# Fixed PSUM pairs with a planned slot per product, and score blocks in two clusters of four, in a two-layer graph attention kernel

## The chip, the cores and the metric

The kernel runs on one core of a Trainium2 chip (trn2). The metric is the device time of one execution in microseconds. The kernel before took 2311.61 us, the median of three runs (2310.8 to 2316.13).

## What is computed

64 graphs of 256 nodes with 512 features go through two layers, all in fp32. Cut to what matters, for one graph:

```
# layer 0
p = x @ fc_w.T + fc_b
l = (p @ q_w + q_b)[:, None] + (p @ k_w + k_b)[None, :]
l = leaky_relu(l + (1 - adj) * -1e9, 0.01)
x = softmax(l) @ p + x
# layer 1, 8 heads of 64, the layer's "adjacency" is the same adj
Q, K, V = x @ W_q + b_q, x @ W_k + b_k, x @ W_v + b_v
s = Q K^T / 8 + (x @ w_g[:D])[:, None] + (x @ w_g[D:])[None, :] + b_g + log(adj + 1e-9)
out = softmax(s) V + x
```

## The kernel before

**Groups and steps.** Two graphs make a group (512 tokens, four tiles of 128), so there are 32 groups and 32 steps. The function `step` (its pieces are strings such as `"pq.p7 pq.p2"`) works on four groups at once: `f` is the group whose layer 0 ends and whose projections to Q, K and V are made; `a` is the group before it, in its attention; `d` is the one before `a`, whose second graph is finished; `n` is the next one, which is loaded and whose layer-0 weights are made. The order of the pieces in these strings is the order in which each engine gets its instructions: a manual schedule keeps it, and every engine runs its queue in order. So the strings in `attention_and_layer_0` and `step` are what decides which instruction stands behind which.

**Products.** Each 512 x 512 x 512 product (`pq`, `pk`, `pv` for the projections, `pf` for layer 0) is made of seven products of blocks, `p1` to `p7` (class `Product`, `add` at L412). One block product is four matmuls of 128x256 with a contraction of 128; the profile shows two records for each fp32 matmul, so 8 records. `p1`, `p2` and `p7` start a new PSUM bank (`fresh`); `p6`, `p5` and `p3` add to `p1`'s bank, and `p4` adds to `p7`'s. Between them the bank is read: `keep_1`, and the `keep` inside `p6` and `p5`, copy it on ScalarE (L429, or L432 as two halves with a bias; for `pf` L494 as two halves with a factor, followed by an addition on GpSimd, L495). `p3`'s result is read by ScalarE (for `pf` by VectorE). `sum_00`, `sum_11` and `sum_10` read a bank on VectorE (L443; for `pf` L501).

**Layer 0.** `mix:0` to `mix:3` make `y` (L689), four products of 8 records, each copied to SBUF by ScalarE (L695). `recip` makes row sums on TensorE (L637). `residual` (L830) is four ScalarE instructions that prepare x plus the bias for the output; `turn_residual` turns it on VectorE.

**Attention.** `scores:u` for u = 0 to 3 (one graph and four of its heads each) makes two score blocks, jc = 0 and 1, one for each 128 of the graph's nodes. A block is four matmuls (L859) with a contraction of 64, two at a time on the two halves of the array's rows; it fills two banks, and one exp on ScalarE (L873) reads both. `factor:u:jc` multiplies the exp by the adjacency on VectorE (L879), `both:u` adds the two blocks (L886). `attend:gr` makes V times weights for one graph (L899): two halves of 8 matmuls with 64 output columns, two at a time on halves of the array's columns; each half fills one bank, which ScalarE copies (L906). `totals_0` is a small matmul for the sums (L927).

**PSUM before.** There are eight banks. Four of them turn in a pool of single banks (`ps`, 4 buffers), which every block product, `y` and `attend` takes from in order of need; the other four are a pool of two pairs (`psc`), which the score blocks and `pq.p7` take in turn:

```
def bank(name):
    return ps.tile([P, 512], F32, tag="bank", name=name)

def pair(name):
    return psc.tile([P, 2, 512], F32, tag="pair", name=name)
```

The framework sets the waits between engines from what each instruction reads and writes, tile by tile.

**Order before, around the attention.** On TensorE: `pv.p5`, `scores:0`, `attend:1` (of `d`), `scores:1`, `pv.p3`, `pv.p4`, `mix:0`, `mix:1`, `recip`, `mix:2`, `mix:3`, `pf.p1`, `p2`, `p6`, `p7`, `p5`, `p3`, `scores:2`, `attend:0`, `totals_0`, `scores:3`, `pf.p4`, then `pq.p1`, `pk.p1`, `pv.p1`, `pq.p6`, `p7`, `p2`, `p5`, `pk.p6`, `pq.p3`, `p4`, `pk.p7`, `p5`, `p2`, `p3`, `p4`, `pv.p2`, `p6`, `p7`, `p5`.

Of the kernel before, what the change touches and what calls it, by code (L numbers as in the profile page):

```python
# [17 lines left out]
P = 128  # L18
# [7 lines left out]
def kernel(  # L26
# [119 lines left out]
    def transposed_weights(w, pool, psum, copy):  # L146

        t = pool.tile([P, NC, D], F32, tag="fcT", name="fcT")
        for hc in range(NC):
            pt = psum.tile([P, 512], F32, tag="bank", name=f"pfc_{hc}")  # L150
            for oc in range(NC):
                nc.tensor.transpose(pt[:, ts(oc, P)], w[:, oc, ts(hc, P)], ident)
            copy(t[:, hc, :], pt)
        return t
# [9 lines left out]
    def fast():  # L164
        main = ExitStack()
        with main:
# [6 lines left out]
                tc.tile_pool(name="ps", bufs=4, space=bass.MemoryType.PSUM)  # L173
            )
            psc = main.enter_context(
                tc.tile_pool(name="psc", bufs=2, space=bass.MemoryType.PSUM)
            )

            def bank(name):
                return ps.tile([P, 512], F32, tag="bank", name=name)  # L180

            def pair(name):
                return psc.tile([P, 2, 512], F32, tag="pair", name=name)
# [61 lines left out]
            def columns(rows, cols, name):  # L245

                n = rows.shape[0]
                pt = bank(name)
                nc.tensor.transpose(pt[:, 0:n], rows, ident[0:n, 0:n])
                nc.vector.tensor_copy(cols, pt[:, 0:n])  # L250
# [6 lines left out]
            def rows_of_x():  # L257

                pr = bank("rows_qk")[0:2, :]
                for oc in range(NC):  # L260
                    nc.tensor.matmul(
                        pr, lhsT=cols_0[:, oc : oc + NC + 1 : NC], rhs=fc_nat[:, oc, :],
                        start=(oc == 0), stop=(oc == NC - 1),
                    )
                rows = one.tile([2, D], F32, tag="junk", name="rows_qk_sb")
                nc.scalar.copy(rows, pr)
                return rows

            def spread_rows(rows):

                for n, dst in enumerate((wq_row, wk_row)):
                    pt = bank(f"row_{n}")
                    nc.tensor.matmul(
                        pt, lhsT=ident[0:2, n : n + 1].to_broadcast([2, P]), rhs=rows,
                        start=True, stop=True,
                    )
                    nc.scalar.copy(dst, pt)

            def constant():

                both = two.tile([P, NC], F32, tag="c", name="qk_col")
                part = two.tile([P, 2, T], F32, tag="kq", name="qk_fcb")
                nc.vector.tensor_tensor(both, qw_col, kw_col, ALU.add)
                nc.vector.tensor_tensor(both, both, fcb_col, ALU.mult)
                nc.vector.tensor_reduce(part[:, 0, 0:1], both, AX.X, ALU.add)
                pk = bank("pk")
                nc.tensor.matmul(
                    pk[:, 0:1], lhsT=part[:, 0, 0:1].to_broadcast([P, P]), rhs=ones[:, 0, 0:1],
                    start=True, stop=True,
                )  # L290
                return lambda: nc.vector.scalar_tensor_tensor(
                    kqc, pk[:, 0:1], qb, kb, ALU.add, ALU.add
                )

            def constants_of_projections():


                pc = bank("pc")[:, 0:HALF]
# [11 lines left out]
                def add():  # L310
                    pt = bank("pct")
# [77 lines left out]
            class Product:  # L389
# [5 lines left out]
                scores = False  # L395

                def __init__(self, name, a, b, out, rows, bias=None):
                    self.name, self.a, self.b, self.out = name, a, b, out
                    self.rows, self.bias = rows, bias
# [18 lines left out]
                def fresh(self, n, scores=False):  # L418
                    name = f"{self.name}_{n}"
                    dst = (pair(name)[:, 0] if scores else bank(name)).rearrange(  # L420
                        "p (m k) -> p m k", m=2
                    )
                    self.add(n, dst, True)
                    return dst
# [36 lines left out]
                def p7(self):  # L461
                    self.r2 = self.fresh(7, self.scores)
# [66 lines left out]
            class Group:  # L529


                older = None

# [43 lines left out]
                def queries(self):  # L577

                    pt = bank(f"qrow_{self.g}")
# [52 lines left out]
                def recip(self):  # L632
# [3 lines left out]
                    all_sums = bank(f"rc_{self.g}")[:, 0:ALL]  # L636
# [15 lines left out]
                def sums(self):  # L652

                    sm = bank(f"sm0_{self.g}")[:, 0:P]
# [10 lines left out]
                def recip_of_sums(self):  # L665
                    pt = bank(f"rc_{self.g}")[:, 0:P]
                    nc.tensor.transpose(pt, self.sms, ident)
                    nc.vector.reciprocal(
                        recip0[:, self.g, :], pt.rearrange("p (t r) -> p t r", t=T)[:, :, 0]
                    )  # L670

                def mix(self, c):
# [13 lines left out]
                    y = bank(f"y_{g}_{c}")  # L686
# [10 lines left out]
                def features_first(self):  # L697
# [4 lines left out]
                    for t in range(T):  # L702
                        pt = bank(f"xTp_{g}_{t}")
# [7 lines left out]
                    fcT = transposed_weights(fc_nat, wts, ps, nc.scalar.copy)  # L711
# [3 lines left out]
                    def product(t):  # L715
                        pp = bank(f"fp_{g}_{t}")
# [29 lines left out]
                    for t in range(T):  # L746
                        gr, ic = divmod(t, TPG)
                        po = bank(f"x1p_{g}_{t}")
# [16 lines left out]
                def begin(self):  # L765
# [19 lines left out]
                    self.pq.scores = True  # L785
# [21 lines left out]
                def x1t(self, t):  # L807

                    pt = bank(f"x1Tp_{self.g}_{t}")
# [37 lines left out]
                def scores(self, u):  # L847
# [5 lines left out]
                    for jc in range(TPG):  # L853
                        t = gr * TPG + jc
                        sc = pair(f"sc_{g}_{u}_{jc}").rearrange("p a (b i) -> p a b i", b=2)
# [32 lines left out]
                def attend(self, gr):  # L888
# [3 lines left out]
                    for hg in range(2):  # L892
                        po = bank(f"oT_{g}_{gr}_{hg}")
# [40 lines left out]
                def totals_1(self):  # L934
                    self.totals(1, bank(f"tot_{self.g}_1")[:, 0 : NC * N // B])

                def totals_0(self):
                    self.totals(0, bank(f"tot_{self.g}_0")[:, 0 : NC * N // B])
# [16 lines left out]
                def sums_1(self, gr):  # L955
# [3 lines left out]
                    sm = bank(f"sm_{g}_{gr}")[:, 0:N]  # L959
# [11 lines left out]
                def sums_of_e(self, gr):  # L971

                    g = self.g
                    sm = bank(f"sm_{g}_{gr}")[:, 0:N]
# [93 lines left out]
            def attention_and_layer_0(D, A, F, X):  # L1068

                A("scores:0")  # L1070
                D("attend:1")
                F("add_tiles")
                A("scores:1 factor:0:0 factor:0:1 pv.sum_11 pv.p3 pv.p4")
                D("turn:1")
                F("parts_0")
                A("factor:1:0 factor:1:1 pv.sum_10 both:0 both:1")
# [8 lines left out]
                A("scores:2 attend:0 totals_0")  # L1085
                F("pf.sum_01 send:0:1 fetch:1:1 fetch:0:1")
                F("copy:0")
                A("factor:2:0 factor:2:1 scores:3 turn:0 ratios:0 both:2")
                F("pf.p4 pf.sum_10 send:1:0 fetch:1:0")
                F("pq.p1 pq.keep_1 pk.p1 pk.keep_1 pv.p1 pv.keep_1")  # L1090

            def check_ranges():

                in_range(NG - NR // 2, NG, "last")
                pk = bank("pok")
# [11 lines left out]
            def step(d, a, f, n, check):  # L1107
# [24 lines left out]
                A("factor:3:0 factor:3:1 both:3")  # L1132
# [18 lines left out]
                if n is None:  # L1151
                    A("attend:1 totals_1 ratios:1 turn:1 divide:1 complete:1 store:1")
# [17 lines left out]
            with tc.manual_schedule(engines=ENGINES):  # L1170
# [3 lines left out]
                warm = bank("warm")  # L1174
# [17 lines left out]
    def general(pool):  # L1192
# [12 lines left out]
        with tc.tile_pool(name="gwps", bufs=2, space=bass.MemoryType.PSUM) as wps:  # L1205
            fcT = transposed_weights(fc_nat, pool, wps, nc.vector.tensor_copy)
# [199 lines left out]
```

## Time and profile before

| what | value |
|---|---|
| time, median of 3 runs (range) | 2311.61 us (2310.8 to 2316.13) |
| span of the profiled execution | 2308.8 us |
| TensorE busy, matmul records | 2294.2 us (99%), 12618 records |
| VectorE busy | 2124.2 us (92%) |
| ScalarE busy | 1071.8 us (46%) |
| GpSimd busy | 121.9 us (5%) |
| mean granted TensorE clock | 0.997 |
| HBM read and written over the span | 70 GB/s |

The span runs from the first to the last instruction of one execution; the times of the runs have what is outside the span as well, some 2.8 us. Busy time is the union of an engine's records. PE is TensorE's matmuls, PEld its weight loads, DVE VectorE, ACT ScalarE, POOL GpSimd, SP the engine that issues most DMAs. In a line of the timeline the columns are: start, length (both us), engine, line of the kernel, operation, what is written <- what is read, shapes, number of instructions merged, and in square brackets the idle time of that engine before it and what ended it. Ends of matmuls are modelled and reach over the start of the next one, so the distance of two starts, not the length, is a matmul's price.

### The profile page before, as it was taken

How to read it: one execution, taken by the hardware profiler on the slowest of the kernel's cores; microseconds unless marked ns; L12 is line 12 of the kernel's file. 1: busy time of each engine (PE TensorE's matmuls, PEld its weight loads, DVE VectorE, ACT ScalarE, POOL GpSimd, SP SyncE). 2: the span in 40 equal slices, each digit the busy share in tenths (PEclk: the TensorE clock that was granted, in tenths of full speed). 3: DMA queues.
4: the chain of work that ended last, by engine and by line, in shares of the span. 5: the costliest groups of instructions: out<-in, count | busy, mean ns of one | idle time of the engine just before them, and what ended most of it. 6: DMA issues, size and time to landing. Idle time of an engine off the chain costs nothing.

```text
span 2308.8 us, 33613 instructions
## 1 busy us (share of the span) xinstructions
PE 2294.2 (99%) x12618; PEld 1905.2 (83%) x12618; DVE 2124.2 (92%) x3180; ACT 1071.8 (46%) x1865; POOL 121.9 (5%) x120
## 2 busy tenths in 40 slices
PE   9999999999999999999999999999999999999997
PEld 6888888888888888888888888888888888888885
DVE  6899999999999999999999999999999999999997
ACT  3544444454445444454444454444544445444443
POOL 0000000000000000000000000000000000000000
PEclk9999999999999999999999999999999999999999
DMA  4122332223322233232233232332222323223312
GB/s 133 46 61 73 78 76 66 70 61 85 79 73 61 61 78 78 74 68 61 69 78 83 60 75 63 79 78 74 64 60 74 78 73 70 65 64 81 84 46 38
DMA packets 517264, 163.84 MB, mean 71 GB/s; under 512 B 415188, under 2 KB 478696, under 8 KB 517096
## 3 DMA queue, kind: packets, MB, share of 16 engines
q1 hardware_dynamic: 514440, 160.32, 28.8%
q8 instruction: 102, 1.67, 0.3%
q10 hardware_dynamic: 2656, 1.31, 0.2%
q14 instruction: 66, 0.54, 0.1%
HBM read 95.43 MB, written 66.12 MB: 70 GB/s over the span
## 4 chain that ended last, share of the span: by engine, by line
PE 98%; DVE 1%; DMA 0%; ACT 0%; issue 0%; ACTq 0%; DVEq 0%
PE pv L412 17%; PE pq L412 17%; PE pf L412 16%; PE pk L412 16%; PE sc L859 11%; PE oT L899 10%; PE y L689 9%; PE fp L718 1%; DMA fc_nat<-in_L_gnn_fc_w_dram 0%; PE rc L637 0%; DVE osb L1034 0%; PE tot L927 0%; DVE osb L1040 0%; PE xTp L705 0%; DVE osb L1033 0%; DVE x L756 0%
## 5 line engine op out<-in xcount | busy, mean ns | idle before, releaser
L873 ACT ACTIVATE e<-sc,c 128x1024 f32<-128x1024 f32 x254 | 269.0, 1110 | 79.2 <-PE sc L859 77.6
L879 DVE TENSOR_TENSOR e<-e,am 128x1024 f32<-128x1024 f32 x254 | 297.7, 1213 | 0.4 <-ACT e L873 0.4
L859 PE MATMUL sc<-qT,kT 64*128 64x256 f32 x2048 | 255.8, 390 | 0.3 <-ACT e L873 0.3
L899 PE MATMUL oT<-e,v 128*64 128x256 f32 x2032 | 233.4, 382 | 0.0
L859 PEld LDWEIGHTS sc<-qT,kT 64*128 64x128 f32 x2048 | 187.3, 187 | 52.6 <-issue 32.7
L495 POOL TENSOR_TENSOR pf_s<-pf_s,x 128x512 f32<-128x512 f32 x93 | 118.4, 1273 | 2106.1 <-ACT pf_s L494 2038.8
L689 PE MATMUL y<-e,x 128*128 128x256 f32 x992 | 225.6, 381 | 0.0
L899 PEld LDWEIGHTS oT<-e,v 128*64 128x64 f32 x2032 | 140.2, 137 | 85.3 <-issue 10.7
L689 PEld LDWEIGHTS y<-e,x 128*128 128x128 f32 x992 | 186.4, 190 | 23.7
L432 ACT ACTIVATE pq_s<-pq,cols 128x256 f32<-128x256 f32 x192 | 80.5, 470 | 249.1 <-PE pq L412 249.1
L494 ACT ACTIVATE pf_s<-pf,recip 128x256 f32<-128x256 f32 x186 | 77.9, 470 | 197.6 <-PE pf L412 197.6
L917 DVE TENSOR_REDUCE part<-est 128x32 f32<-128x1024 f32 x124 | 151.3, 1220 | 4.3
L916 DVE STREAM_TRANSPOSE est<-es 128x1024 f32<-128x1024 f32 x124 | 152.2, 1227 | 0.0
L886 DVE TENSOR_TENSOR es<-e,e 128x1024 f32<-128x1024 f32 x126 | 149.3, 1205 | 1.1
L695 ACT COPY yT<-y 128x512 f32<-128x512 f32 x124 | 72.6, 585 | 131.7 <-PE y L689 130.9
L429 ACT COPY pk_s<-pk 128x512 f32<-128x512 f32 x96 | 56.3, 586 | 165.7 <-PE pk L412 159.0
L906 ACT COPY oTs<-oT 128x512 f32<-128x512 f32 x128 | 75.0, 586 | 118.0 <-PE oT L899 97.3
L412 PE MATMUL pk<-t1b,wk 128*128 128x256 f32 x512 | 121.1, 380 | 0.4 <-DVE kT L443 0.4
L412 PE MATMUL pv<-wv,t1b_c 128*128 128x256 f32 x512 | 121.1, 380 | 0.0
L412 PE MATMUL pv<-wv,t1b 128*128 128x256 f32 x512 | 121.0, 380 | 0.0
L412 PE MATMUL pq<-x1T,wq 128*128 128x256 f32 x512 | 121.0, 379 | 0.0
L412 PE MATMUL pk<-x1T,wk 128*128 128x256 f32 x512 | 121.0, 379 | 0.0
(181 smaller groups left out, 4506.3 us busy)
## 6 DMA issues: line engine op xcount, KB each, us to landing
x<-in_x_dram SPq DMA_DIRECT2D x32, 1024.0 KB, 5.1
out_dram<-osb SPq DMA_DIRECT2D x254, 128.0 KB, 3.1
xd<-xt SPq DMA_DIRECT2D x124, 256.0 KB, 2.0
x1T<-xd SPq DMA_DIRECT2D x496, 64.0 KB, 1.9
adj<-in_adj_dram SPq DMA_DIRECT2D x128, 128.0 KB, 3.5
qrow<-q SPq DMA_DIRECT2D x31, 256.0 KB, 3.9
fc_nat<-in_L_gnn_fc_w_dram ACTq DMA_DIRECT2D x4, 256.0 KB, 3.8
wq<-in_L_gnn_W_q_dram SPq DMA_DIRECT2D x1, 1024.0 KB
```

The costliest lines, as they stand in the source:

```text
L412: nc.tensor.matmul(o, lhsT=lk[:, ts(m, P)] if len(lk.shape) == 2 else lk[:, m], rhs=rk, start=(start and m == 0 and k == 0), stop=(m == 1 ...
L432: nc.scalar.activation(dst[:, m], src[:, m], AF.Identity, bias=self.bias[:, 2 * o + m : 2 * o + m + 1],)
L494: nc.scalar.mul(s[:, m], src[:, m], self.recip[:, TPG * k + m : TPG * k + m + 1])
L495: nc.gpsimd.tensor_tensor(s, s, self.out(o, k), ALU.add)
L689: nc.tensor.matmul(y[:, ts(gr, N)], lhsT=self.x[:, gr * TPG + j, ts(c, P)], rhs=self.e0[:, j, gr, :], start=(gr == 0 and j == 0), stop=(gr ...
L859: nc.tensor.matmul(sc[:, par, pr, :], lhsT=self.kT[rows, 2 * hg + pr, ts(t, P)], rhs=self.qT[rows, 2 * hg + pr, ts(gr, N)], start=True, st ...
L873: nc.scalar.activation(e, sc, AF.Exp, bias=self.c[:, t : t + 1], scale=SCALE)
L879: nc.vector.tensor_tensor(ef, ef, self.am[:, jc, u // 2, :].unsqueeze(1).to_broadcast([P, 4, N]), ALU.mult,)
L886: nc.vector.tensor_tensor(self.esum[u], self.e[u, 0], self.e[u, 1], ALU.add)
L899: nc.tensor.matmul(oT[par * HD : (par + 1) * HD, pr, :], lhsT=self.v[:, gr * TPG + jc, ts(h, HD)], rhs=self.e[2 * gr + hg, jc][:, par, pr, :],
L916: nc.vector.transpose(turned, self.esum[u].rearrange("p a b i -> p (a b i)"))
L917: nc.vector.tensor_reduce(self.part[:, hg, :], turned.rearrange("p (m c) -> p m c", c=B), AX.X, ALU.add,)
```

## The change

The pool of four single banks and the pool of two pairs give way to one pool with four fixed tiles of two banks each, X, Y, Z and W. A slot is a half of one of them: Xa, Xb, ... Wb. Each product has its slots by name (`slots`, for `p1`, `p7`, `p2` and `p3`), so have `y` (Za, Zb, Wa, Wb), `attend` (Wa, Wb) and the totals (Ya); score blocks take whole pairs in the order Y, Z, W, Y, X, Z, W, X. What comes before and after the steps takes slots in turn (`FREE`).

In the order, `attend:1` now stands ahead of `scores:0` and `scores:1`, which follow each other; `attend:0` and `totals_0` come before `pf.p4`, and `scores:2` and `scores:3` follow it, one after the other, ahead of `pq.p1`. The VectorE work on the exps moves with them: `factor:2:0` stands behind `pv.keep_1`, and `factor:2:1`, `both:2` behind `pq.p6`, ahead of `factor:3:0`; `add_tiles` and `parts_0` stand together ahead of the scores, and `factor:1:0`, `both:0`, `factor:1:1` behind `pv.p4`. `pf.sum_10`, `send:1:0`, `fetch:1:0` and `copy:0` stand between `scores:2` and `scores:3`.

```diff
             ps = main.enter_context(
-                tc.tile_pool(name="ps", bufs=4, space=bass.MemoryType.PSUM)
+                tc.tile_pool(name="ps", bufs=1, space=bass.MemoryType.PSUM)
             )
-            psc = main.enter_context(
-                tc.tile_pool(name="psc", bufs=2, space=bass.MemoryType.PSUM)
-            )
-            def bank(name):
-                return ps.tile([P, 512], F32, tag="bank", name=name)
-            def pair(name):
-                return psc.tile([P, 2, 512], F32, tag="pair", name=name)
+            pairs = {
+                n: ps.tile([P, 2, 512], F32, tag=f"pair_{n}", name=f"pair_{n}") for n in "XYZW"
+            }
+            FREE = ("Xa", "Xb", "Ya", "Yb", "Za", "Zb", "Wa")
+            turns = [0]
+            def bank(slot=None):
+                if slot is None:
+                    turns[0] += 1
+                    slot = FREE[turns[0] % len(FREE)]
+                return pairs[slot[0]][:, "ab".index(slot[1])]
...
-                scores = False
+                slots = dict(v="Xa Xb Wb", q="Ya Yb Wa", k="Za Zb Ya", fc="Xa Yb Xb Za")
...
+                    self.slot = dict(zip((1, 7, 2, 3), self.slots[a].split()))
...
-                def fresh(self, n, scores=False):
-                    name = f"{self.name}_{n}"
-                    dst = (pair(name)[:, 0] if scores else bank(name)).rearrange(
-                        "p (m k) -> p m k", m=2
-                    )
+                def fresh(self, n):
+                    dst = bank(self.slot[n]).rearrange("p (m k) -> p m k", m=2)
...
+                score_pairs = "YZWYXZWX"
+                attend_slots = 2 * (("Wa", "Wb"),)
+                total_slots = ("Ya", "Zb")
+                sum_slots = ("Wb", "Xa")
...
-                    all_sums = bank(f"rc_{self.g}")[:, 0:ALL]
+                    all_sums = bank("Ya")[:, 0:ALL]
...
-                    y = bank(f"y_{g}_{c}")
+                    y = bank(("Za", "Zb", "Wa", "Wb")[c])
...
-                        sc = pair(f"sc_{g}_{u}_{jc}").rearrange("p a (b i) -> p a b i", b=2)
+                        sc = pairs[self.score_pairs[2 * u + jc]].rearrange(
+                            "p a (b i) -> p a b i", b=2
+                        )
...
-                        po = bank(f"oT_{g}_{gr}_{hg}")
+                        po = bank(self.attend_slots[gr][hg])
...
-                A("scores:0")
                 D("attend:1")
-                F("add_tiles")
-                A("scores:1 factor:0:0 factor:0:1 pv.sum_11 pv.p3 pv.p4")
+                F("add_tiles parts_0")
+                A("scores:0 scores:1 pv.sum_11")
                 D("turn:1")
-                F("parts_0")
-                A("factor:1:0 factor:1:1 pv.sum_10 both:0 both:1")
+                A("factor:0:0 factor:0:1 pv.p3 pv.p4 factor:1:0 both:0 factor:1:1 pv.sum_10 both:1")
...
-                A("scores:2 attend:0 totals_0")
+                A("attend:0 totals_0")
                 F("pf.sum_01 send:0:1 fetch:1:1 fetch:0:1")
-                F("copy:0")
-                A("factor:2:0 factor:2:1 scores:3 turn:0 ratios:0 both:2")
-                F("pf.p4 pf.sum_10 send:1:0 fetch:1:0")
+                F("pf.p4")
+                A("ratios:0 turn:0 scores:2")
+                F("pf.sum_10 send:1:0 fetch:1:0 copy:0")
+                A("scores:3")
                 F("pq.p1 pq.keep_1 pk.p1 pk.keep_1 pv.p1 pv.keep_1")
+                A("factor:2:0")
...
-                A("factor:3:0 factor:3:1 both:3")
+                A("factor:2:1 both:2 factor:3:0 factor:3:1 both:3")
...
                 if n is None:
+                    f.score_pairs = 4 * "YZ"
+                    f.attend_slots = (("Wa", "Wb"), ("Ya", "Yb"))
+                    f.pv.slot[2] = "Xb"
```

## The prediction, on record before the changed kernel ran

> **What bounds the kernel now.** I read the busy times first, then the chain of work that ended last, then the timeline of one step (1000 to 1075 us), then who waited for whom.
>
> ```profile
> PE 2294.2 (99%) x12618; PEld 1905.2 (83%) x12618; DVE 2124.2 (92%) x3180; ACT 1071.8 (46%) x1865; POOL 121.9 (5%) x120
> ...
> PE 98%; DVE 1%; DMA 0%; ACT 0%; issue 0%; ACTq 0%; DVEq 0%
> ```
>
> TensorE is the bound. In the timeline a product of 8 records follows the next every 1.73 us (216 ns a record) without a gap, so whatever keeps TensorE waiting in a step is added to the time in full. The next lines are evictions: products, and the ScalarE reads that empty their banks.
>
> ```profile
> 1005.67 3.62 PE L689 MATMUL y<-e,x 128*128 128x256 f32 x16
> ...
> 1007.59 0.59 ACT L695 COPY yT<-y 128x512 f32<-128x512 f32 x1 [2.87 <-PE y L689]
> ...
> 1010.47 1.70 ACT L830 ACTIVATE xv<-x1T,cols 128x256 f32<-128x256 f32 x4
> ...
> 1012.20 0.58 ACT L695 COPY yT<-y 128x512 f32<-128x512 f32 x1
> ...
> 1037.81 3.62 PE L412 MATMUL pq<-t1b,q_s 128*128 128x256 f32 x16
> ...
> 1039.73 0.84 ACT L432 ACTIVATE pq_s<-pq,cols 128x256 f32<-128x256 f32 x2 [1.10 <-PE pq L412]
> ```
>
> See that the x16 lines hold two products: the second starts (1007.40, 1039.54) before ScalarE has even begun to read the first. It can, for each product has a bank of its own. What a change between kinds of matmul costs (TensorE alone):
>
> ```profile
> 1021.43 1.89 PE L412 MATMUL pf<-fc_s,yT 128*128 128x256 f32 x8
> 1023.25 2.00 PE L859 MATMUL sc<-qT,kT 64*128 64x256 f32 x16
> 1025.18 3.67 PE L899 MATMUL oT<-e,v 128*64 128x256 f32 x32
> 1028.68 0.26 PE L927 MATMUL tot<-part,every 128*64 128x32 f32 x4
> 1028.87 2.00 PE L859 MATMUL sc<-qT,kT 64*128 64x256 f32 x16
> 1030.80 2.00 PE L412 MATMUL pf<-fcT,tb 128*128 128x256 f32 x8
> ```
>
> And what a real wait costs; both are rare in the kernel before, one near the end and one in the first attention:
>
> ```profile
> 2259.99 1.89 PE L412 MATMUL pk<-x1T,k_s 128*128 128x256 f32 x8
> 2262.30 1.99 PE L412 MATMUL pk<-t1b,wk 128*128 128x256 f32 x8 [0.42 <-DVE kT L443]
> ```
>
> ```profile
> 77.40 2.12 ACT L873 ACTIVATE e<-sc,c 128x1024 f32<-128x1024 f32 x2
> ...
> 78.56 2.14 PE L859 MATMUL sc<-qT,kT 64*128 64x256 f32 x16 [0.35 <-ACT e L873]
> ```
>
> The first exp ends at 77.40 + 1.11 (its row's mean) = 78.51; TensorE resumes 0.05 us later. And the product after a wait takes 1.99 us, not 1.89: 0.10 more, a weight load that nothing covers.
>
> **What the Trainium skill says.** "TensorEngine Tiling (Array Packing)", Key Properties: changing the tiling mode drains TensorE. The trace agrees: about 0.2 us a change (below). "Perfetto Trace Analysis", Matmuls: independent groups should rotate through different PSUM banks, so that evacuation overlaps the next group's matmuls. That is the second fence. "PSUM — Partial Sum Buffer", PSUM bank collisions: what must be kept apart is a bank and a 32-partition quadrant; different banks may be used at once. The trace agrees: from 1039.73 ScalarE reads pq's one bank while TensorE writes its other. The changed program waits more coarsely than that. "TensorE: Matmul & The Clock Gate", What's actually happening: the clock falls after an idle window of about 3.4 us. The 0.8 us wait at 2262.30 was followed at the old pace (1.99, then 1.73 a product), so I assume full clock.
>
> **The change, part by part.**
>
> *Two clusters.* From the third fence, before a step costs: product to scores 0.20 (0.09 at the boundary, 0.10 inside the cluster), scores to attend 0.15, attend to scores 0.20, scores to product 0.20; then 0.20, 0.15, totals to scores 0.20, 0.20. Sum 1.50. After: product to attend 0.14 (the last attend shows it at 2264.22), attend to scores 0.20, scores to product 0.20; then product to attend 0.14, totals to product 0.20 (seen at 2267.91), product to scores 0.20, scores to product 0.20. Sum 1.28. Gain 0.2 us a step, in the 30 steps that have an older group: **-6 us**. It is no more because attend, too, is another tiling mode, and the second attend now stands alone between products.
>
> *The pairs.* Each pair is now one PSUM tile, where a bank was one. The built program shows what follows: an instruction that writes one half waits for the instruction that empties the *other* half. So the second `y` of a pair waits for the copy of the first, the second half of an attend for the copy of its first half. I counted waits of a TensorE instruction on an eviction which itself waits for the product directly before: none in the steps before (at the nearest, a whole product lies between), and in the steps of the changed program 316: the second and fourth `y` (31 each), pf.p2 (31), pq.p7, pq.p4, pk.p4 (32 each), pv.p7 (31), pv.p4 (32), both attends (64). Behind each waits all of TensorE, which runs in order, and behind that everything. Costs:
> - One copy: TensorE would go on at 1007.40; the copy ends at 1008.18, plus 0.05 to resume, plus 0.10: 0.93. Second `y`, pk.p4, pv.p7, pv.p4: 126 x 0.93 = 117.2. For pv.p4 the cluster's four exps are in front of that copy on ScalarE: the first starts 1.18 us into the cluster (1000.18 to 1001.36), they follow at 1.01 and end at 5.3, before pv.p3 can be read at 3.66 + 1.83 + 0.19 = 5.7.
> - Fourth `y`: ScalarE first does the residual (L830), so the third's copy starts at 1012.20, although the third product (from 1009.30, 1.77 long) ended its turn at 1011.07: 1012.83 - 1011.07 + 0.10 = 1.86. 31 x 1.86 = 57.7.
> - Two half-bank reads, 0.84 in all: 1039.73 + 0.84 + 0.05 - 1039.54 + 0.10 = 1.18. pf.p2, pq.p7, pq.p4: 95 x 1.18 = 112.1.
> - Attend: its copy starts 0.22 after the next matmul would (1028.90 against 1028.68), takes 0.58, then 0.05, and a 0.05 shorter weight load: 0.90. 64 x 0.90 = 57.6.
>
> Sum **344.6**.
>
> *Waits on VectorE by the same cause.* pf.p5 waits for sum_00, which waits for keep_2: 1.73 + 0.19 + 0.84 + 0.87 + 0.05 after p6's start, against 3.46: 0.22 + 0.10 = 0.32 (0 to 0.8), x31 = 10. pq.p3 waits for sum_11: 1.73 + 0.19 + 0.84 + 0.68 + 0.05 = 3.49 after p5: 0.03 + 0.10, I take 0.2 (0 to 1.0), x32 = 6. pk.p3 waits for pk.sum_11, which before ended at 1056.03 against p3's 1055.07; VectorE has the same work in a longer step, so I take 0.15 (0 to 1.1), x32 = 5. attend:1 waits for pv.sum_00, before 1066.82 against 1065.53; I take 0.1 (0 to 0.5), x30 = 3. Sum **24** (0 to 107).
>
> *Costed at nothing.* factor:2:0 to 3:1 come later on VectorE; attend:1, which needs them, is over 20 us away, and VectorE at 2124 of some 2680 us falls to 79%. In a cluster the fourth block reuses the first's pair: the first exp ends 0.22 + 1.11 us after its block, plus 0.05, and two blocks (1.73) lie between. copy:0 sits behind an exp, its reader pv.p1 two products later. pf.p4 is earlier, so its DMAs start earlier on SP. If a cover fails it is some 0.3 to 1 us a step, as in the upper ends.
>
> *Start and end.* 13 such waits before and after the steps, mostly beside other waits: 5 (0 to 10).
>
> Total: -6 + 344.6 + 24 + 5 = 368 on the span of 2308.8, so 2676.4. The median of the three runs, 2311.61, lies 2.8 us above that span, for what is outside it; so the forecast is **2679**.
>
> **Rivals.** (1) *The waits are met when TensorE gets there; only the clusters count.* Time: 2311.6 - 6 = 2305, not slower. For it: banks are apart on the chip. Against: the wait is in the instruction, and the read it names starts 0.19 us after TensorE would be ready. It decides only if the mean cost of the 316 is under 6 / 316 = 0.02 us, where I read 0.9 to 1.9. Even if both boundaries of two clusters were saved, 0.4 x 2 x 31 = 25 us, 0.08 us a wait would eat it. (2) *VectorE and ScalarE lag as well*: the upper ends of pk.p3, pq.p3, pf.p5 and attend:1, 107 - 24 = 83 us more: 2762. For it: VectorE was 1 us late at pk.p3 before. Against: it gains 11 us of slack a step. (3) *Half of the waits are covered*, by late products or reads already made: 2679 - 184 = 2495. Nothing in the order speaks for it. (4) *The clock falls* with the idle time, 14% of the step: no wait summed here reaches 3.4 us; I fold it into (2).
>
> **How the numbers follow.** As summed 0.85, (2) and (4) 0.08, (3) 0.04, (1) 0.03. The sum's lower end, without VectorE's waits and with the fourth `y` at 0.93, is 2679 - 24 - 29 = 2626; its upper end is (2). Range 2626 to 2762. Within 0.3% is about what this measurement cannot tell from no change: of (1), 0.02 lie there and 0.01 below; the rest is slower.
>
> **What would show it.** TensorE's busy share falls to about 89% (the records' ends reach 0.16 us past the next one's start, so the idle shown is that much less than the loss); new idle in front of the second and fourth `y`, pf.p2, pq.p7, pq.p4, pk.p4, pv.p7, pv.p4 and the second half of each attend, 0.7 to 1.6 us each, ended by ScalarE's reads; a step, 70.9 us before (pk's long run starts at 199.46 and 270.33), grows to about 82.5. Scores lines of x32 twice a step. If TensorE stays at 99% busy, the waits cost nothing and I am wrong by all of it; if the idle is ended by VectorE, by (2)'s share.

## The result, and the profile after

The changed kernel took 2704.77 us (median of 4 runs, 2703.85 to 2705.66); the kernel before took 2312.19 us beside it (median of 4). The ratio is 1.17 [1.1683, 1.1716]: slower by 393 us. The forecast was 2679 us, range 2626 to 2762: the side and the mechanism were right, the time 26 us too low.

The page of the changed kernel, busy times and the chain of work that ended last:

```profile
PE 2396.7 (89%) x12618; PEld 1873.1 (69%) x12618; DVE 2143.6 (79%) x3180; ACT 1062.5 (39%) x1865; POOL 121.9 (5%) x120
...
PE 74%; ACT 11%; DVE 7%; issue 5%; DMA 2%; SPq 1%; DVEq 0%; ACTq 0%; POOL 0%; POOLq 0%
```

The same 12618 matmul records now fill 89% of the span, and ScalarE holds 11% of a chain in which it had 0%. The span is 2703.9 us, the granted clock 0.996. The timeline of TensorE alone through one step shows where the idle time sits (start and length in us; in square brackets the idle time before the line and what ended it):

```profile
1182.34 1.99 PE L694 MATMUL pair_Z<-e,x 128*128 128x256 f32 x8 [0.68 <-ACT yT L700]
...
1184.35 1.93 PE L694 MATMUL pair_W<-e,x 128*128 128x256 f32 x8
1187.89 1.99 PE L694 MATMUL pair_W<-e,x 128*128 128x256 f32 x8 [1.61 <-ACT yT L700]
1189.72 1.89 PE L416 MATMUL pair_X<-fcT,yT 128*128 128x256 f32 x8
1192.54 1.99 PE L416 MATMUL pair_X<-fcT,yT 128*128 128x256 f32 x8 [0.93 <-ACT pf_s L495]
...
1198.25 1.96 PE L416 MATMUL pair_X<-fcT,tb 128*128 128x256 f32 x8 [0.26 <-DVE x L502]
...
1201.87 1.95 PE L905 MATMUL pair_W<-e,v 128*64 128x256 f32 x16
1204.55 1.95 PE L905 MATMUL pair_W<-e,v 128*64 128x256 f32 x16 [0.73 <-ACT oTs L912]
1206.32 0.26 PE L933 MATMUL pair_Y<-part,every 128*64 128x32 f32 x4
1206.51 1.99 PE L416 MATMUL pair_Y<-fcT,tb 128*128 128x256 f32 x8
1208.43 1.13 PE L865 MATMUL pair_X<-qT,kT 64*128 64x256 f32 x8
...
1212.09 1.99 PE L416 MATMUL pair_Y<-x1T,wq 128*128 128x256 f32 x8
...
1264.94 1.99 PE L694 MATMUL pair_Z<-e,x 128*128 128x256 f32 x8 [0.68 <-ACT yT L700]
```

Lines that held two products (x16) before are now two lines with a gap. Second `y`: 1182.34 to 1264.94, a step of 82.60 us, where the kernel before had 70.88. The fourth `y` (1187.89) has the widest gap. The cluster of four score blocks (1208.43 to 1212.09) has none; its 32 records stand in four lines of x8, each under the name of its pair, and not in one line of x32 as the prediction had it. ScalarE's lines say why the fourth `y` is late:

```profile
1184.37 0.58 ACT L700 COPY yT<-pair_Z 128x512 f32<-128x512 f32 x1 [2.08 <-PE pair_Z L694]
...
1185.52 1.71 ACT L834 ACTIVATE xv<-x1T,cols 128x256 f32<-128x256 f32 x4
1187.25 0.58 ACT L700 COPY yT<-pair_W 128x512 f32<-128x512 f32 x1
```

The third `y` is finished near 1186.1, but its copy stands behind the residual (L834) and starts at 1187.25; TensorE goes on when that copy has ended. The view of waits, TensorE alone (waited for; us in total, times, longest):

```profile
PE pair_W L694 <- ACT yT L700: 49.7, 31, 1.6
PE pair_W L905 <- ACT oTs L912: 44.6, 63, 0.7
PE pair_Y L416 <- ACT qT L433: 29.7, 32, 0.9
PE pair_Y L416 <- ACT pq_s L433: 29.7, 32, 0.9
PE pair_X L416 <- ACT pf_s L495: 28.8, 31, 0.9
PE pair_X L416 <- ACT v L430: 21.6, 32, 0.7
PE pair_Z L416 <- ACT kT L430: 21.6, 32, 0.7
PE pair_Z L694 <- ACT yT L700: 20.9, 31, 0.7
PE pair_X L416 <- ACT pv_s L430: 20.9, 31, 0.7
PE pair_X L416 <- DVE x L502: 8.1, 31, 0.3
PE pair_Z L416 <- DVE kT L444: 4.9, 5, 2.2
```

The first nine rows are 315 waits of the forecast's list of 316, each at its place and ended by ScalarE's read of the other half of the same pair (the last, an attend in pair Y, is a row of its own). The kernel before has none of these nine.

Where the 395.1 us of span (2308.8 to 2703.9) lie, by the starts of the row sums (`recip`, one in every step but the first): 20.2 before the first one (87.64 to 107.87), 358.0 in the 30 intervals between them, 16.8 after the last (94.8 to 111.6). Of the 358.0, 30 x 11.72 = 351.6 are the common step; 6.4 are single steps that are longer, up to 84.04.

### The profile page after: what moved, and what is told of

It reads as the page before. It is cut to its first block, busy times and chain, and to the rows that moved or that the text cites. A ratio compares the mean times of both kernels' runs of the same rounds, so it can differ in the third digit from the quotient of the medians.

```text
span 2703.9 us, 33681 instructions
## 1 busy us (share of the span) xinstructions
PE 2396.7 (89%) x12618; PEld 1873.1 (69%) x12618; DVE 2143.6 (79%) x3180; ACT 1062.5 (39%) x1865; POOL 121.9 (5%) x120
## 4 chain that ended last, share of the span: by engine, by line
PE 74%; ACT 11%; DVE 7%; issue 5%; DMA 2%; SPq 1%; DVEq 0%; ACTq 0%; POOL 0%; POOLq 0%
PE pair_X L416 21%; PE pair_Y L416 15%; PE pair_Z L416 12%; PE pair_W L905 7%; PE pair_Z L694 4%; PE pair_W L416 4%; PE pair_W L694 2%; PE pair_Y L865 2%; ACT xv L834 2%; ACT pf_s L495 2%; PE pair_X L865 2%; PE pair_Z L865 2%; PE pair_W L865 2%; ACT yT L700 2%; DVE x L502 1%
## 5 line engine op out<-in xcount | busy, mean ns | idle before, releaser
L905 PE MATMUL pair_W<-e,v 128*64 128x256 f32 x2016 | 245.8, 386 | 44.6 <-ACT oTs L912 44.6
L905 PEld LDWEIGHTS pair_W<-e,v 128*64 128x64 f32 x2016 | 133.7, 137 | 151.1 <-ACT oTs L912 73.3
L694 PE MATMUL pair_W<-e,x 128*128 128x256 f32 x496 | 121.8, 388 | 49.7 <-ACT yT L700 49.7
L416 PE MATMUL pair_Y<-t1b,wq 128*128 128x256 f32 x512 | 124.3, 386 | 29.7 <-ACT qT L433 29.7
L416 PE MATMUL pair_Y<-t1b,q_s 128*128 128x256 f32 x512 | 124.3, 386 | 29.7 <-ACT pq_s L433 29.7
L416 PE MATMUL pair_X<-fcT,yT 128*128 128x256 f32 x496 | 120.4, 386 | 28.8 <-ACT pf_s L495 28.8
L416 PE MATMUL pair_Z<-t1b,wk 128*128 128x256 f32 x512 | 126.1, 390 | 21.6 <-ACT kT L430 21.6
L416 PE MATMUL pair_X<-wv,t1b 128*128 128x256 f32 x512 | 124.4, 386 | 21.6 <-ACT v L430 21.6
L416 PE MATMUL pair_X<-v_s,t1b 128*128 128x256 f32 x512 | 124.4, 386 | 20.9 <-ACT pv_s L430 20.9
L694 PE MATMUL pair_Z<-e,x 128*128 128x256 f32 x496 | 120.4, 386 | 20.9 <-ACT yT L700 20.9
```

The lines of the kernel that those rows point to most:

```text
L416: nc.tensor.matmul(o, lhsT=lk[:, ts(m, P)] if len(lk.shape) == 2 else lk[:, m], rhs=rk, start=(start and m == 0 and k == 0), stop=(m == 1 ...
L694: nc.tensor.matmul(y[:, ts(gr, N)], lhsT=self.x[:, gr * TPG + j, ts(c, P)], rhs=self.e0[:, j, gr, :], start=(gr == 0 and j == 0), stop=(gr ...
L905: nc.tensor.matmul(oT[par * HD : (par + 1) * HD, pr, :], lhsT=self.v[:, gr * TPG + jc, ts(h, HD)], rhs=self.e[2 * gr + hg, jc][:, par, pr, :],
```

## The experiments

Two theories. The one on record: the time comes of the pairs as tiles, since an instruction on one half waits for the reader of the other half (A in most expectations below). The rival: it comes of the new order, or of a VectorE or ScalarE that the new order makes late. All times are medians; the kernel before, run beside each of them on the same chip, took 2310.9 to 2312.1 us.

### The same slots and order, but eight tiles of one bank (e1_single)

```diff
-            pairs = {
-                n: ps.tile([P, 2, 512], F32, tag=f"pair_{n}", name=f"pair_{n}") for n in "XYZW"
-            }
+            banks = {
+                n + h: ps.tile([P, 512], F32, tag=f"bank_{n}{h}", name=f"bank_{n}{h}")
+                for n in "XYZW" for h in "ab"
+            }
...
-                return pairs[slot[0]][:, "ab".index(slot[1])]
+                return banks[slot]
...
-                        nc.scalar.activation(e, sc, AF.Exp, bias=self.c[:, t : t + 1], scale=SCALE)
+                        for par in range(2):
+                            nc.scalar.activation(
+                                e[:, par], sc[par], AF.Exp, bias=self.c[:, t : t + 1], scale=SCALE
+                            )
```

A score block then has two tiles, and its exp is two instructions.

> The changed kernel, order and slots as they are, but each of the eight banks is a PSUM tile of its own instead of half of a pair; each score block's exp is therefore two instructions of 128x512 instead of one of 128x1024. Theory A (waits that reach over to the other half of a pair cost all of the 392 us): they are gone, the two clusters' 6 us remain, 2306 us (2300 to 2312), TensorE back at 99% busy. Theory B (the new order costs a good part, by VectorE's work on the exps coming later and attend standing in front of the scores): 2340 us or more, with TensorE idle ended by VectorE.

Measured: 2327.46 us, ratio 1.007 [1.0056, 1.0083]. 377 of the 393 us are gone by the grain of the tiles (with the exps that it splits), with every product in the same bank and the same place in the order. That settles the main question; e3_y and e4_replan below confirm it with the pairs and whole exps kept. But theory A expected 2306; some 16 us over the kernel before are left, and they are ended by VectorE (chain, then waits of the weight loads and of VectorE):

```profile
PE 62%; DVE 25%; DMA 8%; issue 2%; SPq 2%; DVEq 0%; ACT 0%; ACTq 0%
```

```profile
PEld bank_Zb L417 <- DVE kT L445: 16.6, 28, 1.3
PEld bank_Wb L910 <- DVE v L445: 14.7, 30, 0.5
```

They sit at pk.p4 (12.9 us of lost pace) and at the second half of `attend:1` (7.3 us). So the rival has a small share, of which more below.

### The pools of before, the new order (e2_order)

The edit is the order part of the diff alone, on the pools of the kernel before.

> The kernel before with its own two PSUM pools, and only the new order of the pieces (two clusters of four blocks, factor, parts and pf.p4 moved). With two pairs in the pool the third block of a cluster waits for the first's exp (ready 2.34 us into the cluster, needed at 1.83, and 0.10 for a weight load) and the fourth for the second's (0.05 and 0.10): 0.76 us a cluster, 62 clusters, 47 us, less the 6 us of the switch. Theory A: about 2353 us (2335 to 2370), all new idle in front of score blocks and ended by ScalarE's exps. Theory B: 2400 us or more, with idle at other products too.

Measured: 2358.55 us, ratio 1.0206 [1.019, 1.0222], 48 us slower than the kernel before (forecast 41). TensorE's timeline:

```profile
1161.65 2.00 PE L859 MATMUL sc<-qT,kT 64*128 64x256 f32 x16
1163.99 2.14 PE L859 MATMUL sc<-qT,kT 64*128 64x256 f32 x16 [0.35 <-ACT e L873]
```

Two pairs can't hold a cluster of four blocks: the third and fourth wait for the exps of the first and second. The common step is 72.20 us, 1.32 more than before, which is the sum forecast (2 x 0.76, less 0.20). Some 5 us more lie in single longer steps, where TensorE waits for VectorE at pk.p4 and in `attend:1`, the places of e1_single's waits; theory A had nothing of these. The wait for the exps is a cost of the order that the changed kernel does not pay, since three pairs serve its clusters; it can't be what made the changed kernel slow.

### The four `y` products in alternate pairs (e3_y)

```diff
-                    y = bank(("Za", "Zb", "Wa", "Wb")[c])
+                    y = bank(("Za", "Wa", "Zb", "Wb")[c])
```

> The changed kernel, with the four y products in the order of slots Za, Wa, Zb, Wb instead of Za, Zb, Wa, Wb, so that a y waits for the copy of the one before the last. Theory A: the second y's 0.93 us and the fourth's 1.86 us go, 31 x 2.79 = 86 us, 2618 us (2610 to 2628). Theory B, or ScalarE being late anyway (the residual's four instructions stand in front of the third copy): the idle moves to pf.p1 or pf.p2 and less than 40 us is gained, 2665 us or more.

Measured: 2618.25 us, ratio 1.1328 [1.1311, 1.1346]: 86.5 us less than the changed kernel, from two exchanged names. The step falls by 2.82 us to 79.78; the forecast's terms for the second and fourth `y` are 0.93 + 1.86 = 2.79.

### And more products away from their neighbours' pairs (e4_replan)

On top of e3_y:

```diff
-                slots = dict(v="Xa Xb Wb", q="Ya Yb Wa", k="Za Zb Ya", fc="Xa Yb Xb Za")
+                slots = dict(v="Xa Xb Wb", q="Ya Wa Wb", k="Za Yb Wa", fc="Xa Yb Zb Za")
...
-                attend_slots = 2 * (("Wa", "Wb"),)
+                attend_slots = (("Wa", "Wb"), ("Za", "Wa"))
```

> As the one before, and the other slots chosen so that neighbours on TensorE are in different pairs where that can be: pq in Ya, Wa, Wb, pk in Za, Yb, Wa, pf in Xa, Yb, Zb, Za, the second attend in Za, Wa. Left are pv.p7, pv.p4 and the first attend (2.76 us a step). Theory A: gains y 86, pq.p7 and pq.p4 76 (with pq.p3 82), pk.p4 and pk.p3 35, pf.p2 and pf.p5 47, attend 28, in all 278 us: 2427 us (2410 to 2445). Theory B: 2460 us or more.

Measured: 2414.26 us, ratio 1.0446 [1.043, 1.0462]; the step is 73.60 us. Three waits a step were left in (pv.p7, pv.p4, one half of an attend), and the waits of this kernel are those:

```profile
PE pair_W L905 <- ACT oTs L912: 23.4, 32, 0.7
PE pair_X L416 <- ACT v L430: 21.6, 32, 0.7
PE pair_X L416 <- ACT pv_s L430: 20.9, 31, 0.7
```

The other ScalarE rows of the changed kernel's list are gone. The cost goes wait by wait, as a sum.

### Another turn of the slots before and after the steps (e7_free)

```diff
-            FREE = ("Xa", "Xb", "Ya", "Yb", "Za", "Zb", "Wa")
+            FREE = ("Xa", "Ya", "Za", "Wa", "Xb", "Yb", "Zb")
```

> The changed kernel (pairs), with the banks of the start taken in turn from different pairs: Xa, Ya, Za, Wa, Xb, Yb, Zb instead of Xa, Xb, Ya, Yb, Za, Zb, Wa. The trace has the first row sums at 107.9 us, 20.2 later than in the kernel before, of which the steps' own waits explain some 6. Theory A: the other 14 are the 13 waits between neighbours at the start, at full price; they go: 2704.8 - 13 = 2692 us (2688 to 2696). Rival: those waits lie beside VectorE's and the DMAs' (my forecast's 0.4 us each): 2700 us.

Measured: 2687.44 us, ratio 1.1629 [1.1611, 1.1647], 17.3 us less than the changed kernel and a little more than expected. The first row sums start at 93.75 instead of 107.87 (14.1 us), and the part after the last one is 108.5 instead of 111.6 (3.1 us). Not all of it is waits. At the start TensorE has nine waits fewer, of about 1 us each. But also, the granted clock was 0.50 from 14.0 to 24.3 us in the changed kernel's profiled execution and 1.00 there in that of e7_free; half of the time in which matmuls ran in that stretch, some 4 us, is my estimate of what this cost. And the 3.1 us at the end are not e7_free's doing, as the changed kernel's TensorE shows:

```profile
2648.00 2.70 PE L416 MATMUL pair_Z<-x1T,k_s 128*128 128x256 f32 x8 [2.22 <-DVE kT L444]
2651.38 3.78 PE L416 MATMUL pair_Z<-t1b,wk 128*128 128x256 f32 x8 [0.68 <-ACT kT L430]
```

After the wait of 2.22 us a product takes 3.71 us to the start of the next line (2655.09), where the same product takes 1.92 in e12_keysa below: half pace. The mean granted clock was 0.51 from 2649.1 to 2656.0, which costs about 3 us. e7_free has the same wait in its last step, and no such stretch behind it. So of the 17.2 us at start and end of the two profiled executions some 10 are waits between neighbours, as the forecast priced them, and some 7 go with the clock. Whether the waits at the start brought the slow clock there is not shown.

### What is left in e1_single: a wrong guess (e5_sums, e6_p4)

I first put e1_single's 16 us down to two pieces of VectorE work that stand too late at the waits seen. e5_sums moves them:

```diff
-                score_pairs = "YZWYXZWX"
-                attend_slots = 2 * (("Wa", "Wb"),)
+                score_pairs = "YWZYXZWX"
+                attend_slots = (("Wa", "Wb"), ("Wa", "Za"))
...
-                A("complete:0 store:0 parts:2")
+                A("complete:0 store:0")
+                F("pk.p7 pk.p5 pk.sum_11 residual:0")
+                A("parts:2")
                 if n is None:
                     A("parts:3")
-                F("pk.p7 pk.p5 pk.sum_11 residual:0")
```

> The kernel with eight single banks and the new order, and two edits against the two stalls that its trace showed: parts:2 stands behind pk.sum_11 on VectorE (pk.p4 waited for that sum, 12.9 us in all), and the second attend's halves take Wa and Za, with the score blocks in Y, W, Z, Y (its second half in Wb waited for pv.sum_00, which reads Wb, 7.3 us in all). Theory A2 (the single-bank kernel missed its 2306 us only by VectorE being late at these two places): 2327 - 12.9 - 7.3 = 2307 us (2302 to 2312), just faster than the kernel before. Theory B2 (VectorE's later work on the exps binds elsewhere when these are gone): 2315 us or more, with the idle at other sums.

Measured: 2366.94 us, ratio 1.0241 [1.0227, 1.0255]. The waits moved and grew: TensorE now waits at pq.p3 and pf.p4 (the first and the second row).

```profile
PE bank_Ya L417 <- ACT pq_s L434: 36.8, 30, 1.9
PE bank_Yb L417 <- DVE x L503: 8.4, 20, 0.5
```

e6_p4 moves pf.p4, with its sum, its send and its fetch, behind `scores:3` on top of that:

```diff
-                F("pf.p4")
                 A("ratios:0 turn:0 scores:2")
-                F("pf.sum_10 send:1:0 fetch:1:0 copy:0")
+                F("copy:0")
                 A("scores:3")
+                F("pf.p4 pf.sum_10 send:1:0 fetch:1:0")
```

> As the one before, and pf.p4 with its sum, send and fetch behind scores:3 instead of ahead of scores:2, so that the first attend, the totals and the second cluster follow each other and one change of tile mode less is paid in 31 steps: 31 x 0.2 = 6 us less than its neighbour, 2301 us by theory A2. By B2 (pf.sum_10 and its DMAs are later by 3.9 us, and pq.p2 waits for them) no gain, or a loss of up to 2 us a step.

Measured: 2380.18 us, ratio 1.0295 [1.0281, 1.0309]: worse again, with the wait at pq.p3 as before and a new one at the cluster's second block. So moving the sums was not the remedy. The chain of e5_sums says what I should have read first:

```profile
DVE 63%; PE 14%; DMA 10%; issue 9%; SPq 3%; ACT 0%; DVEq 0%; ACTq 0%
```

TensorE is no longer the bound there: VectorE with its DMAs is. The question is then what VectorE itself waits for, not who waits for VectorE.

### What VectorE waits for (e8_keys, e10_load, e9_keys5)

The waits of VectorE in e1_single, top three rows:

```profile
DVE jq L521 <- DMA x<-in_x_dram: 45.1, 30, 2.0
DVE t1b L379 <- DMA x1T<-xd: 24.2, 31, 2.4
DVE e L890 <- ACT e L882: 22.7, 31, 0.7
```

In the kernel before, the first of these is 14.2 us; the other two are 0.4 us each, once. One step of VectorE in e1_single:

```profile
1108.34 1.23 DVE L890 TENSOR_TENSOR e<-e,am 128x1024 f32<-128x1024 f32 x1 [0.73 <-ACT e L882]
1110.01 0.69 DVE L379 TENSOR_TENSOR t1b<-x1T 128x512 f32<-128x512 f32 x1 [0.45 <-DMA x1T<-xd]
...
1117.87 0.69 DVE L521 CUSTOM_DVE_ANT_0 jc<-x,wgc_row 128x512 f32<-128x512 f32 x1
...
1126.08 0.69 DVE L521 CUSTOM_DVE_ANT_0 jq<-x,wq_row 128x512 f32<-128x512 f32 x1 [1.47 <-DMA x<-in_x_dram]
```

`keys` (jc) is the last reader of the one x buffer, so the next x is loaded behind it, 1 MB with 5.1 us from issue to landing; `dot_q` (jq) needs it. And `t1b` waits for x1T, which comes back through the buffer xd by `send` and `fetch`. The new order moved `factor:2:1` and `both:2` from in front of `t1b` to between `t1b` and `keys`: the wait at `t1b` lost its cover, and the load starts later. The edit, on e1_single:

```diff
                 A("scores:3")
                 F("pq.p1 pq.keep_1 pk.p1 pk.keep_1 pv.p1 pv.keep_1")
+                F("keys:2 keys:3 keys:0 keys:1")
+                X("load_x")
                 A("factor:2:0")
...
                 A("factor:2:1 both:2 factor:3:0 factor:3:1 both:3")
-                F("keys:2 keys:3 keys:0 keys:1")
-                X("load_x")
+                if a is None:
+                    F("keys:2 keys:3 keys:0 keys:1")
+                    X("load_x")
```

> e1_single with the four products of keys (VectorE, L521, 0.77 us each with the read of its sum) and the load of the next x behind them moved ahead of factor:2:0 and of the sums t1b, so that they run while VectorE waits for the transposed x1. Theory A: the 15 us that e1_single lost against the kernel before are a VectorE that sits idle for two transfers which the order of before covered with factors of the later score blocks, the x load (45.1 us of waits at jq) and the return of x1T (24.2 us at t1b). With both covered TensorE no longer waits for VectorE at pk.p4 and at the second attend: 2307 to 2312 us, VectorE's waits at jq and t1b together under 25 us. Theory B: VectorE is late because of where its work lies, not because of its idle time: 2322 us or more, also if the two waits go.

Measured: 2304.69 us, ratio 0.9969 [0.9958, 0.998]: faster than both kernels by a little, below the range expected, and 22.8 us under e1_single. VectorE and the chain of e8_keys:

```profile
1098.61 0.65 DVE L521 CUSTOM_DVE_ANT_0 jc<-x,wgc_row 128x512 f32<-128x512 f32 x1
...
1102.53 0.68 DVE L379 TENSOR_TENSOR t1b<-x1T 128x512 f32<-128x512 f32 x1
...
1115.61 0.68 DVE L521 CUSTOM_DVE_ANT_0 jq<-x,wq_row 128x512 f32<-128x512 f32 x1
```

```profile
PE 98%; DVE 1%; DMA 0%; issue 0%; SPq 0%; ACT 0%; DVEq 0%
```

No idle time ahead of `t1b` or `jq` in this step; in the whole run VectorE waits 1.6 us for the fetched x1T and never for x at `jq`. Every step is 70.673 us, 0.20 under the 70.878 of the kernel before.

e10_load moves the same two lines only ahead of `factor:2:1`, behind the sums `t1b`: the x load is covered, the return of x1T is not.

> e1_single with keys and the x load moved only ahead of factor:2:1 to both:3, behind the sums t1b: this covers the x load and leaves the wait for x1T as it is. Theory A: the 45.1 us at jq fall to about 10, the 24.2 us at t1b stay; two thirds of VectorE's lost time come back, 2310 to 2318 us. Theory B: 2322 us or more.

Measured: 2308.24 us, ratio 0.9988 [0.9982, 0.9995]. VectorE's wait at `jq` is gone, the one at `t1b` stays:

```profile
DVE t1b L379 <- DMA x1T<-xd: 25.5, 31, 2.3
```

So the x load is most of it (19.2 of 22.8 us), a little more than expected. The other 3.6 us go with the wait at `t1b` and with that of `factor:2:0` for its exp, which is 22.7 us here as in e1_single and gone in e8_keys; these runs do not tell the two apart. e9_keys5 is the move of e8_keys on e5_sums.

> e5_sums (2366.9 us) with the same move of keys and of the x load. Theory A: the wait at pq.p3 (about 48 us with what follows it) comes of the 73 us that VectorE waited at t1b and the 51 us at jq; with keys between the send and the sums it is mostly gone: 2307 to 2330 us. Theory B: pq.sum_00 stands as late as before because VectorE's queue ahead of it is as long: 2350 us or more.

Measured: 2305.13 us, ratio 0.9973 [0.9961, 0.9984], 61.8 us under e5_sums and below the range expected; VectorE's waits at `t1b` fall from 73.2 to 3.8 us, those at `jq` from 51.1 to none. With the two transfers covered, the other edits of e5_sums cost nothing (0.4 us against e8_keys).

### The same move in the two original kernels (e11_keysb, e12_keysa)

> The kernel before (its pools, its order) with the same move of keys and of the next x load, ahead of the sums t1b. Theory A: TensorE there waits for VectorE hardly anywhere, so covering VectorE's 14.2 us at jq brings nothing: 2309 to 2313 us, ratio 0.999 to 1.001, and the 6.6 us by which e8_keys beats the kernel before come of the clusters (122 changes of tiling mode at about 0.05 us or so fewer) and not of the move. Rival: the move itself brings them, 2304 to 2307 us.

Measured on the kernel before: 2341.5 us, ratio 1.0129 [1.0113, 1.0144]. Both theories missed. In that order nothing waits at `t1b`, and the sums come just in time for pq.p6; with the four `keys` ahead of them (2.8 us) they are late:

```profile
1124.38 3.69 PE L412 MATMUL pq<-t1b,q_s 128*128 128x256 f32 x16 [0.75 <-DVE t1b L375]
```

The step is 0.98 us longer, every time. So this run does not tell what the 6.6 us of e8_keys come from. The traces do. In the common step of the kernel before and of e8_keys TensorE waits for nothing, and from product to product the distances are the same (1.73 us). They differ only where the kind of matmul changes. e8_keys:

```profile
1095.03 1.99 PE L417 MATMUL bank_Yb<-fcT,tb 128*128 128x256 f32 x8
1096.95 0.48 PE L867 MATMUL bank_Xa<-qT,kT 64*128 64x256 f32 x1
...
1100.61 1.99 PE L417 MATMUL bank_Ya<-x1T,wq 128*128 128x256 f32 x8
```

Four score blocks take 3.66 us here (1096.95 to 1100.61) and 3.86 as twice two blocks before (1023.25 to 1025.18 and 1028.87 to 1030.80), 0.41 less in the two clusters of a step by the unrounded starts. pf.p4 (1095.03), which now stands between the totals and the scores, takes 1.92 to the next start instead of 1.83, and the product behind the cluster 1.83 instead of 1.73: 0.20 more. The difference is the 0.20 us a step, 6.2 of the 6.6 us in 30 steps.

> The changed kernel (pairs) with the same move. Theory A: the sporadic waits at pk.p3 (5 to 6 us beyond the usual 0.1, VectorE's pk.sum_00 late) are the part of the changed kernel that comes of VectorE's order; they go, the 316 waits on the other half of a pair stay: 2694 to 2700 us. Rival: no part of the 393 us comes of VectorE's order: 2703 to 2706 us.

Measured on the changed kernel: 2698.82 us, ratio 1.1677 [1.1661, 1.1693], 6.0 us less. Of the five waits of TensorE on VectorE at pk.p3 (L444) with 4.9 us in all, one is left, that of the last step:

```profile
PE pair_Z L416 <- DVE kT L444: 2.2, 1, 2.2
```

The intervals between the row sums lose 4.5 us of the 6.4 that single steps were over the common one. In the profiled execution the part after the last row sums is 3.2 us shorter as well; that is the stretch at half clock behind 2648.00, which this execution does not have, and not the move. The waits on the pairs are as before (49.7, 44.7 and 29.7 us in the first three rows).

## Why the prediction was right, and where it was too low

**What bounds the kernel, and the pairs.** Right. The price of a wait is read from the timeline as the distance of the late product's start from the start before it, less the ordinary 1.73 us, plus what the late product's own first weight load adds (0.10 behind ScalarE's waits, or 0.05 with 64 columns).

| term | forecast, us each | measured |
|---|---|---|
| second `y`, pk.p4, pv.p7, pv.p4 (126) | 0.93 | 0.84 + 0.10 = 0.94 |
| fourth `y` (31) | 1.86 | 1.77 + 0.10 = 1.87 |
| pf.p2, pq.p7, pq.p4 (95) | 1.18 | 1.09 + 0.10 = 1.19 to 1.20 |
| second half of attend (64) | 0.90 | 0.85 to 0.90 + 0.05 = 0.90 to 0.95 |
| pf.p5 (31) | 0.32 | 0.42 + 0.08 = 0.50 |
| pq.p3 (32) | 0.2 | 0.09 + 0.10 = 0.19 in most steps, up to 0.5 in some, 1.4 in one |
| pk.p3 (32) | 0.15 | 0.08 in most steps, 0.5 to 1.2 in four, about 2.5 in the last |
| attend:1 (30) | 0.1 | 0.06 |

The sum of 344.6 for the ScalarE waits stands: with the column of measured values it is about 350. e3_y (86.5 us for two of its terms, 31 x 2.79 = 86.5 forecast) and e1_single (377 us for all) show by removal that it is these waits.

**Where the 26 us are.** On the span the forecast was 27.5 us short (2676.4 against 2703.9); the median lies 1.9 us nearer to its span than I had assumed, which leaves 26. (The 2.8 us "for what is outside" the span set a median against the span of one fast execution; every run listed with its span is 1.7 to 1.9 us longer than that span.) These terms were mis-sized:

- *Start and end*, forecast at 5 (0 to 10): I called their waits "mostly beside other waits". They are not; e7_free takes 17.3 us away by turning the slots: +12. In the profiled executions some 7 of these 17 go with stretches at half clock, for which the forecast had nothing.
- *Waits on VectorE*, forecast at 24: pf.p5 took 0.18 more in 31 steps (+5.5). pq.p3 in its common size is as forecast, pk.p3 and attend:1 are a little cheaper (-3). Single steps in which pq.p3 or pk.p3 waits longer add 6.4, of which e12_keysa shows that 4.5 us come of VectorE's late order.
- *Waits on ScalarE*: each 0.01 to 0.05 dearer than its price (+5).

Together +26 of the 27.5 on the span; the rest is open. One reading was wrong as well: the wait at 2262.30 is called 0.8 us, but by its own two lines it is 2262.30 - 2259.99 - 1.73 = 0.58. No term of the sum uses it; it was the ground for assuming full clock.

**The clusters.** -6 fits what e8_keys shows: 0.20 us a step, where 0.22 was summed. The changed kernel has it too: its cluster takes the same 3.66 us (1208.43 to 1212.09), and pf.p4 ahead of it the same 1.92.

**Costed at nothing.** Nearly right for the changed kernel (e12_keysa finds 4.5 to 6 us), and for the reason given (VectorE at 79%), but this cover was the pairs' own waits. With single banks it is gone, and the moved factors cost 22.8 us (e1_single against e8_keys), 0.73 a step, inside the 0.3 to 1 that I had named as the price of a failed cover. What I had not seen is its place: I looked for who needs the factors, and the cost lay in what they were moved past, the `keys` and with them the load of x.

**The rivals.** (1), that the waits are met on arrival, is out: the 316 waits cost 1.1 us each in the mean (350 / 316, by the measured column). (2), ScalarE and VectorE lagging, had its small share in VectorE. (3), half of the waits covered: none is. (4), the clock: small, but not nothing. The mean is 0.996 with 11% of the span idle. Yet the clock was at half for 6.8 us behind the wait of 2.22 us at 2648.00, and in e5_sums for 3.4 us behind four of the 30 waits at pq.p3, each of these four 1.9 us long. The Trainium skill, "TensorE: Matmul & The Clock Gate", What's actually happening, has the clock fall after an idle window of about 3.4 us. The runs agree only in part. Every profile has one longer wait, of 4.2 to 5.0 us near its end, and the clock is at half behind it each time. But the waits in the steps were shorter, and the clock fell all the same, if seldom: mostly it did not, as the same wait of 2.2 us in e3_y, e7_free and e12_keysa and the 31 waits of 1.6 us here show. So that no wait summed reaches 3.4 us, as the prediction argued, is no proof of full clock. What decides it is not shown.

## What to carry to other kernels

Where products follow each other without a gap, give each its own PSUM tile of one bank: two neighbours in halves of one two-bank tile wait for each other's eviction, here 0.9 to 1.9 us each time, although they are different banks (as tiles of their own, in e1_single, the same banks don't make each other wait). If pairs are needed for a wide read, put neighbours into different pairs, or split the read. And when pieces are moved on an engine, look at the DMAs behind the instructions they are moved past: an engine's wait for a load that starts late shows up further on and on another engine, and moving the late instruction only moves the wait.

## What was not expected of the hardware

Each wait of TensorE on a ScalarE read costs the same 0.104 us beyond the wait itself: the product after it takes 1.83 us to the next start instead of 1.73, the first weight load being uncovered, in some 250 waits with hardly any scatter. With 64-column weights it is 0.05, and at pf.p5 and pk.p3, which wait for VectorE's read, 0.08. A wait ended by a 128x512 copy so costs 0.94 us, 0.36 more than the copy's 0.58.

Reading a score block by two exps of 128x512 instead of one of 128x1024 made ScalarE 39.7 us busier (1102.2 in e1_single against 1062.5 in the changed kernel, 256 more instructions, so some 0.16 us each); ScalarE, at 48% in e8_keys, has room for that.
